# A four-layer block on one core: index tiles loaded ahead of tokens and weights, the tokens of the first two chunks of phase two normalized in SBUF, and first-phase times chosen anew

## The chip, the cores and the metric

One Trainium2 chip, of which the kernel uses one core. The metric is the time of one execution in microseconds (us) on the device; the time of a kernel is the median of its runs. The engines of the core are named as in the profile: PE (matrix products), PEld (PE's weight loads), DVE (vector), ACT (scalar), POOL (GpSimd) and SP (whose queue issues most of the transfers).

## The reference

Four layers over 4096 tokens of 512 channels (two sequences of 2048), each with a layernorm in front and a residual addition behind:

```python
x = x + attn_a(_layernorm(x), W_rvk, W_out, time_decay, time_first)
x = x + ffn(_layernorm(x), lut, gate_idx, up_idx, down_idx)
x = x + mamba(_layernorm(x), in_proj_w, conv_w, conv_b, x_proj_w, dt_proj_w, ...)
x = x + ffn(_layernorm(x), lut, gate_idx, up_idx, down_idx)
```

- `attn_a`: r, v, k = x W_rvk. A scan over the tokens of a sequence keeps, for each channel, a running maximum o and two weighted sums p and q; its output is (A p + B v) / (A q + B) with A and B exponentials of differences to the maximum. The result is sigmoid(r) times that output, times W_out.
- `ffn`: silu(x G) * (x U), times D, where G, U (1376 x 512) and D (512 x 1376) are given as 4-bit indices into a table `lut` of 16 numbers.
- `mamba`: x is projected to 1024 channels and 1024 gates; the channels pass a causal convolution of 4 taps and silu (u); x_proj gives 128 numbers for the step size and 16 each for B and C; delta = softplus(dt_proj); for each channel and each of 16 states h = h exp(delta A) + delta u B, y = sum over states of h C, plus u D; times silu(gate), times out_proj.

## The kernel before

**Two phases.** Phase one (pool context `pa`) does the attention of all tokens in 8 chunks of 512 tokens (TA). Each has 4 channel blocks, so there are 32 units, and each unit ends with the operation `y` (L460 and L461). Phase two (`pb`) does the other three layers in 16 chunks of 256 tokens (TB). Each chunk has a period of 32 slots (SLOTS), one for each pair of 512-element scans (L872). The tokens pass from phase one to phase two through memory, in the tiles `x1d`, which L353 stores and `load_x` (L583) fetches.

**The order is written out by hand.** A `Line` collects steps with a time each and emits them sorted by that time; no scheduler reorders them, so an engine's queue is the order of these times. In phase one the times stand in the dictionary `AA`, in units; `t + AA["y"]` is the place of `y` of unit t. In phase two they stand in `AT`, in slots of chunk w from `t = 32 * w`; w = -1 prepares chunk 0. `Stream` lays the weight tiles of phase two, 18 buffers, 8 slots ahead. Transfers are issued by SP's queue in the order of the program, and an issue that waits holds up those behind it.

**Lookups in phase one.** The feed-forward weights come as 11 tiles of 128 x 1536 indices, and each tile's numbers are looked up once and stored to memory (`wff`).

- Three tiles go through PE: `ix` is loaded (L202), cast to bf16 by ACT (L207, `ixb`); for each of 16 values DVE marks where it stands (L211, tile `one`, three buffers), and PE adds nine products of the mark with `pieces` (L218), which are the table's value, split in three bf16 parts, times the identity. ACT makes the 48 pieces (L193), ahead of everything in the order.
- Eight tiles go through DVE alone by bit arithmetic, 23 operations each (`lookup`, L148 to L177): masks `m` from the index bits, then ands and exclusive ors with the columns of `poly`, into `t` (two buffers), with `g` beside it.

The bits are spread over units -3.02 to 29.13, the marks over -4.09 to 10.75. The attention's own operations on DVE (scans L398, L421, L422; products L401, L420, L425; `y`) stand in between.

**Loads at the start** (SP, in order): lut, the two time columns (L96, L97), the first 512 tokens (L109, 1 MB), the four parts of wrvk (L111), wout (L112), the first `ix` (L202), the first bit tile `m3` (L148).

**The first feed-forward of chunk 0** is done within phase one (`feed_forward`, L282 to L319): it fetches the first 256 tokens from `x1d` into `fx`, normalizes them, and runs the eleven weight tiles through gate and up (PE), silu (ACT), a product (L308, DVE) and down (PE, L313). L318 adds the result, and L319 stores it to `x1d`.

**The passage.** The last channel block's `y`, the output products (L347), the last additions (L351), the stores (L353, L319); then phase two loads its small tensors (L518: conv weights and bias, step bias, D, A_log; the rates from A_log by L519 and L520), `x_proj` (wxp) and `dt_proj` (wdt), in_proj weights (L574) and chunk 0's tokens (L583). It normalizes them (`ln`, L601 to L619), makes the front products (L712), convolution and silu (L722 to L738), the x product (L752; its copies are `bcs` and `dtl`, L755, L757; `bcs` goes through the memory tile `bcd` to be broadcast, L759 and L835), the step sizes (`step_size`, L776 to L815, four quarters of two channel blocks each), gates (L842, L848), decay (L862, ACT), growth (L852, POOL) and the scans (L872), of which POOL folds the states (L882). Chunk 1's first feed-forward ("g1", L659) runs in w = 0, with its own load and layernorm of chunk 1's tokens, placed 5.01 slots before chunk 0's scan begins.

The two entry points of the operations that the change moves are these lines, the loads and the first bit tile:

```python
            line.at(times[0] - 1.0, load)
            line.at(ts[0] - (0.35 if i == 0 else 8.5 * (bt[1] - bt[0])), run, steps)
        ...
            if w == 0:
                line.at(t + AT["g1ln"] - 1.0, load_x, 1)
        ...
            if w == -1:
                line.at(t + AT["frontln"] - 3.0, load_x, 0)
```

Of the kernel before, what the change touches and what calls it, by code (L numbers as in the profile page):

```python
# [8 lines left out]
F32 = mybir.dt.float32  # L9
I32 = mybir.dt.int32  # L10
# [5 lines left out]
P = 128  # L16
# [44 lines left out]
def block_kernel(ctx: ExitStack, tc: tile.TileContext, a: dict, out: bass.AP):  # L61
# [20 lines left out]

    with ExitStack() as pa:
        wpool = pa.enter_context(tc.tile_pool(name="a_w", bufs=1))
# [5 lines left out]
        lp = pa.enter_context(tc.tile_pool(name="a_lut", bufs=1))  # L90
# [17 lines left out]
        first = xp.tile([P, TA // P, C], F32, tag="x", name="x")  # L108
        nc.sync.dma_start(first, a["x"][:TA, :].rearrange("(j p) c -> p j c", p=P))  # L109
        for k in range(KC):  # L110
            nc.sync.dma_start(wrvk[:, k, :], a["w_rvk"][k * P : (k + 1) * P, :])  # L111
        nc.sync.dma_start(wout, a["w_out"].rearrange("(k p) d -> p k d", p=P))  # L112

# [4 lines left out]
        for k in range(4):  # L118
# [5 lines left out]
        AA = dict(k=-1.258, r=-0.633, v=-0.836, head=-1.029, sig=-0.383, top=-0.977, e1=-0.75,  # L124
                  e2=-0.62, state=-0.495, vb=-0.271, car=-0.075, num=0.253, den=0.229, rec=0.247,
                  y=0.413, x=-3.46, stats=-3.029, stat=0.083, each=0.062, copy=0.119, fmul=0.867,
                  opened=-3.355, mean=-2.71, scale=-2.177, turn=-2.106, out=3.964, outs=0.02,
                  add=0.188, bits=(-3.02, 29.13), marks=(-4.09, 10.75), ahead=0.503, ff=(11.44,
                  31.66), ffln=10.705, fgate=0.559, fdown=2.36, times=0.284)
# [10 lines left out]
        def lookup(i):  # L140
# [18 lines left out]
            t = it("t", 2)  # L159
# [24 lines left out]
        wide = wpool.tile([P, NLUT], F32, name="wide")  # L184
        V.tensor_copy(rest, lut)
        pieces = wpool.tile([P, 3, NLUT, P], BF16, name="pieces")
        for q in range(3):
            piece = wpool.tile([P, NLUT], BF16, name=f"piece{q}")
            V.tensor_copy(piece, rest)
            V.tensor_copy(wide, piece)  # L190
            V.tensor_tensor(rest, rest, wide, ALU.subtract)
            for j in range(NLUT):
                S.activation(pieces[:, q, j, :], ident, AF.Copy, scale=wide[:, j : j + 1])  # L193

        def lookup_pe(i, times):
# [13 lines left out]
            def mark(j):  # L209
                box[j] = lp.tile([P, 3 * C], BF16, tag="one", name="one", bufs=3)  # L210
                V.tensor_scalar(box[j], box["ixb"], float(j), None, ALU.is_equal)  # L211
# [9 lines left out]
            def take():  # L221
                t = lp.tile([P, 3 * C], I32, tag="t", name="t", bufs=2)
                for b in range(3):
                    S.copy(t.bitcast(F32)[:, b * C : (b + 1) * C], box["w"][b])
                nc.sync.dma_start(wff[i], t.bitcast(F32))

            line.at(times[0] - 1.0, load)
# [6 lines left out]
        def layernorm(t, n, rows_of, box):  # L234
# [30 lines left out]

            line.at(t + AA["mean"], mean)
            for j in range(n):
                d = AA["each"] * j
                line.at(t + AA["stats"] + AA["stat"] * j, stats, j)
                line.at(t + AA["scale"] + d, scale, j)  # L270
                line.at(t + AA["turn"] + d, turn, j)
                line.at(t + AA["turn"] + d + AA["copy"], copy, j)

        def feed_forward(order, times):
# [41 lines left out]
            def close():  # L316
                for j in range(nj):
                    V.tensor_tensor(box["x"][:, j, :], box["x"][:, j, :], box["po"][j], ALU.add)  # L318
                nc.sync.dma_start(x1, box["x"])  # L319

            line.at(AA["ffln"] + AA["stats"] - 0.5, load)
            layernorm(AA["ffln"], nj, lambda j: box["x"][:, j, :], box)
            for n, t in enumerate(times):
# [4 lines left out]
                line.at(t + AA["fdown"], down, n)  # L328
            line.at(times[-1] + AA["fdown"] + 0.1, close)

        def chunk(ci, t):
# [18 lines left out]
            def add(j):  # L350
                V.tensor_tensor(box["x"][:, j, :], box["x"][:, j, :], box["po", j], ALU.add)  # L351
                if j == TA // P - 1:
                    nc.sync.dma_start(x1d[ci].rearrange("(j p) c -> p j c", p=P), box["x"])  # L353

            if ci:
                line.at(t + AA["x"], load)
            else:
                box["x"] = first
# [110 lines left out]

        cars = {}  # L470
# [11 lines left out]
        for i in range(NBITS):  # L482
            steps, ts = lookup(npe + i), bt[NSTEP * i : NSTEP * (i + 1)]
            line.at(ts[0] - (0.35 if i == 0 else 8.5 * (bt[1] - bt[0])), run, steps)
# [8 lines left out]
    with ExitStack() as pb:  # L493
# [4 lines left out]
        tp = pb.enter_context(tc.tile_pool(name="b_T", bufs=4))  # L498
# [13 lines left out]
        cw = wpool.tile([P, ND, KCONV], F32, name="cw")  # L512
        cb = wpool.tile([P, ND], F32, name="cb")
        dtb = wpool.tile([P, ND], F32, name="dtb")
        dcol = wpool.tile([P, ND], F32, name="dcol")
        acol = wpool.tile([P, ND, NS], F32, name="acol")
        for tl, nm in ((cw, "conv_w"), (cb, "conv_b"), (dtb, "dt_b"), (dcol, "D"), (acol, "A_log")):
            nc.sync.dma_start(tl, a[nm])  # L518
        S.activation(acol, acol, AF.Exp)  # L519
        V.tensor_scalar(acol, acol, -1.0, -1.0 / TINY, ALU.mult, ALU.min)  # L520
        hst = wpool.tile([P, ND, NS], F32, name="hst")
        h0 = wpool.tile([P, ND, NS], F32, name="h0")
        G.memset(hst, 0.0)
# [513 lines left out]
```

## Time and profile before

| | |
|---|---|
| median of 3 runs | 3670.57 us (3670.43 to 3672.81) |
| the profiled execution's own time | 3668.55 us |
| its span in the profile | 3666.7 us |
| PE busy | 3389.0 us, 92% |
| DVE busy | 3215.8 us, 88% |
| POOL busy | 3015.4 us, 82% |
| ACT busy | 2744.4 us, 75% |
| first mark (L211) starts | 21.36 us |
| first `y` (L461) starts | 80.2 us |
| last output addition (L351) ends | 704.2 us |
| first front product (L712) starts | 727.85 us |
| first scan (L872) starts | 789.85 us |

How to read the profile: it is one execution, and its times count from the span's start. A busy share is the time in which an engine executes; issuing transfers and waiting are not in it. The rows of slices cut the span in 40 parts of 91.7 us, and each digit is the busy share of one in tenths. A row of a group gives line, engine, operation, output and inputs with shapes, count, then busy time and mean duration, then the idle time that stood before the group's instructions and what ended it. A row of the order of events gives start, length and the same names.

### The profile page before, as it was taken

How to read it: one execution, taken by the hardware profiler on the slowest of the kernel's cores; microseconds unless marked ns; L12 is line 12 of the kernel's file. 1: busy time of each engine (PE TensorE's matmuls, PEld its weight loads, DVE VectorE, ACT ScalarE, POOL GpSimd, SP SyncE). 2: the span in 40 equal slices, each digit the busy share in tenths (PEclk: the TensorE clock that was granted, in tenths of full speed). 3: DMA queues.
4: the chain of work that ended last, by engine and by line, in shares of the span. 5: the costliest groups of instructions: out<-in, count | busy, mean ns of one | idle time of the engine just before them, and what ended most of it. 6: DMA issues, size and time to landing. Idle time of an engine off the chain costs nothing. (4 is left out here: it accounts for less than half of the span.)

```text
span 3666.7 us, 43341 instructions
## 1 busy us (share of the span) xinstructions
PE 3389.0 (92%) x12577; PEld 2292.7 (63%) x12592; DVE 3215.8 (88%) x4880; ACT 2744.4 (75%) x4870; POOL 3015.4 (82%) x2801
## 2 busy tenths in 40 slices
PE   7898999777999999999999999999999999998698
PEld 3443444365676767676767666676767676766475
DVE  7999999459898989999999999999989898989882
ACT  5566776487787878787888878787878787878661
POOL 2555666358999999999999999999999999999850
PEclk9999999898999999999999999999999999999799
DMA  2121111244656565565656565656565555554441
GB/s 112 41 72 66 58 66 66 89 164 139 192 185 190 183 189 184 179 203 166 216 169 206 168 213 167 209 177 200 176 204 179 190 184 190 187 187 136 137 147 60
DMA packets 266876, 572.49 MB, mean 156 GB/s; under 512 B 29840, under 2 KB 31504, under 8 KB 266640
## 3 DMA queue, kind: packets, MB, share of 16 engines
q1 hardware_dynamic: 266640, 569.73, 47.9%
q8 instruction: 101, 1.65, 0.2%
q14 instruction: 135, 1.11, 0.1%
HBM read 543.14 MB, written 26.48 MB: 155 GB/s over the span
## 5 line engine op out<-in xcount | busy, mean ns | idle before, releaser
L872 DVE TENSOR_TENSOR_SCAN h<-h,db 128x512 f32<-128x512 f32 x1024 | 1252.2, 1223 | 124.1 <-ACT h L862 100.1
L852 POOL TENSOR_TENSOR db<-du,bc 128x1024 f32<-128x1024 f32 x512 | 1206.3, 2356 | 37.1 <-PE y L896 35.5
L862 ACT ACTIVATE h<-dl,acol 128x256 f32<-128x256 f32 x2048 | 955.4, 475 | 302.7 <-DVE hst L875 265.1
L873 DVE TENSOR_TENSOR db<-h,bc 128x512 f32<-128x512 f32 x1024 | 708.0, 691 | 35.9
L882 POOL TENSOR_TENSOR db<-db 128x512 f32<-128x512 f32 x480 | 609.4, 1270 | 0.0
L639 PE MATMUL po<-w,hT 128*128 128x512 f32 x1364 | 600.6, 592 | 0.0
L659 PE MATMUL pg<-xnT,w 128*128 128x256 f32 x2480 | 555.2, 381 | 1.8 <-ACT xnT L619 1.8
L659 PE MATMUL gu<-xnT,w 128*128 128x256 f32 x2480 | 555.7, 379 | 0.0
L659 PEld LDWEIGHTS pg<-xnT,w 128*128 128x128 f32 x2480 | 472.9, 191 | 69.6 <-ACT xnT L619 6.4
L659 PEld LDWEIGHTS gu<-xnT,w 128*128 128x128 f32 x2480 | 472.3, 190 | 69.0 <-issue 6.7
L639 PEld LDWEIGHTS po<-w,hT 128*128 128x128 f32 x1364 | 259.7, 190 | 286.9 <-issue 271.8
L888 POOL TENSOR_TENSOR acc<-db 128x256 f32<-128x256 f32 x480 | 348.4, 726 | 37.7
L376 PE MATMUL ps<-xnT,wrvk 128*128 128x512 f32 x768 | 347.4, 604 | 11.7 <-DVE e L401 9.9
L862 ACT ACT_TABLE_LOAD x206 | 264.3, 1283 | 3.6
L376 PEld LDWEIGHTS ps<-xnT,wrvk 128*128 128x128 f32 x768 | 148.7, 195 | 183.9 <-issue 162.3
L842 PE MATMUL ps<-xnT,w 128*128 128x256 f32 x1024 | 235.6, 384 | 26.6 <-DMA w<-in_in_proj 13.5
L842 PEld LDWEIGHTS ps<-xnT,w 128*128 128x128 f32 x1024 | 196.3, 193 | 70.9 <-DVE x L643 23.0
L712 PE MATMUL ps<-xnT,w 128*128 128x256 f32 x1024 | 236.1, 391 | 1.4 <-ACT xnT L619 1.4
L639 PE MATMUL po<-w,u 128*128 128x512 f32 x512 | 231.8, 601 | 2.1 <-DVE u L919 2.1
L712 PEld LDWEIGHTS ps<-xnT,w 128*128 128x128 f32 x1024 | 200.8, 198 | 36.4 <-ACT h L862 3.3
L437 POOL TENSOR_TENSOR d<-aa,opq 128x512 f32<-128x512 f32 x32 | 58.2, 1818 | 195.7 <-DVE opq L422 183.5
L732 DVE SCALAR_TENSOR_TENSOR ps<-xin,cw,ps 128x256 f32<-128x256 f32 x384 | 187.1, 488 | 26.0 <-ACT ps L726 15.5
(155 smaller groups left out, 5059.9 us busy)
## 6 DMA issues: line engine op xcount, KB each, us to landing
w<-wff SPq DMA_DIRECT2D x1023, 256.0 KB, 2.7
bc<-bcd SPq DMA_DIRECT2D x256, 512.0 KB, 4.2
w<-in_in_proj SPq DMA_DIRECT2D x256, 256.0 KB, 2.7
w<-in_out_proj SPq DMA_DIRECT2D x128, 256.0 KB, 2.7
wff<-t SPq DMA_DIRECT2D x11, 768.0 KB, 3.9
w<-wff SPq DMA_DIRECT2D x11, 768.0 KB, 4.3
x<-in_x SPq DMA_DIRECT2D x8, 1024.0 KB, 5.2
x1d<-x SPq DMA_DIRECT2D x8, 1024.0 KB, 4.3
```

Source lines behind the costliest of these rows:

```text
L376: PE.matmul(ps, lhsT=wrvk[:, k, lo : lo + P], rhs=chunk["xnT"][:, k, :], start=(k == 0), stop=(k == KC - 1))
L639: PE.matmul(po[j], lhsT=lw[:, j * P : (j + 1) * P], rhs=w[i]["w"][:m], start=(i == 0), stop=(i == n - 1))
L659: PE.matmul(to[:m], lhsT=w[:, k, :m], rhs=box["xnT"][:, k, :], start=(k == 0), stop=(k == KC - 1))
L712: PE.matmul(ps[cp][:, j, :], lhsT=wj[:, k, :], rhs=box["xnT"][:, k, :], start=(k == 0), stop=(k == KC - 1))
L732: V.scalar_tensor_tensor(ps[cp][:, j, :], xin[cp][:, j, i : i + TB], cw[:, c, i : i + 1], ps[cp][:, j, :], ALU.mult, ALU.add)
L842: PE.matmul(ps[:, j, :], lhsT=wj[:, k, :], rhs=box["xnT"][:, k, :], start=(k == 0), stop=(k == KC - 1))
L852: G.tensor_tensor(d, box["du", half][:, c4, :].unsqueeze(1).to_broadcast([P, 4, TB]), bs[half, q], ALU.mult)
L862: S.activation(h[:, n, :], box["dl", half][:, c4, :], AF.Exp, scale=acol[:, 4 * half + c4, col : col + 1])
L872: V.tensor_tensor_scan(flat(h), flat(h), flat(d[:, two, :]), 0.0, ALU.mult, ALU.add)
L873: V.tensor_tensor(d[:, two, :], h, cs[half, q][:, two, :], ALU.mult)
L882: G.tensor_tensor(d[:, 0:2, :], d[:, 0:2, :], d[:, 2:4, :], ALU.add)
L888: G.tensor_tensor(to, d[:, 0, :], d[:, 1, :], ALU.add)
```

## The change

- **Loads at the start.** The first bit tile (time -9.9 units) and the first index tile (-9.8) are loaded right after the time columns; the first 512 tokens (-9.7), wrvk, wout (-9.6 on) and phase two's small tensors (-9.5) follow. The rates are computed at unit 3.
- **Pieces.** The 48 pieces are no longer made ahead: `place(j)` makes the three of value j at times from -4.5 units on, 0.069 apart, so that the cast stands after the first of them.
- **Buffers of phase one.** `one` has 2 buffers (3 before), `t` of the bits has 1 (2 before), and a PE lookup's result goes back into its index tile. Pool `a_lut` is opened ahead of the other pools of phase one.
- **Times of phase one.** All of `AA` is chosen anew: `den` at -0.133 units (0.229 before), output products 4.08 (3.964), their additions 0.096 later (0.188), bits from -4.21 (-3.02), scaling 0.191 after the mean (0.533), feed-forward from 13.35 (11.44).
- **Hand-over.** A pool `head` that both phases share holds two tiles `ready` (and the small tensors). Phase one normalizes and transposes chunk 1's tokens into `ready[1]` (at unit 7.821, with a load of its own from `x1d`). It normalizes chunk 0's, after its feed-forward's last addition, out of `fx` into `ready[0]`. The last silu, the last product with D, the additions, the statistics and the scaling stand ahead of or beside the last output products; the transposes come behind these. The stores of `fx` and of the last 512 tokens are issued by ACT's queue instead of SP's.
- **Phase two.** Chunk 0's front and chunk 1's first feed-forward take `ready` and skip their own load and `ln`; `front` writes its normalized tokens into `ready[ci % 2]` from then on, and the pool `b_T` has 2 buffers (4 before). wxp and wdt are loaded at the time of the first front product. Chunk 0's tokens, for the residual, are loaded at slot 0. Chunk 0's front, x product and step sizes have times of their own (`fronta`, `xa`, `step0a`); `g1`, `g1s`, `late` and `step1a` are new. All other times of `AT` stay.

The diff, cut:

```diff
+    head = ctx.enter_context(tc.tile_pool(name="head", bufs=1))
+    ready = [head.tile([P, KC, TB], F32, name=f"ready{i}") for i in range(2)]
+    cw = head.tile([P, ND, KCONV], F32, name="cw")
...
     with ExitStack() as pa:
+        lp = pa.enter_context(tc.tile_pool(name="a_lut", bufs=1))
         wpool = pa.enter_context(tc.tile_pool(name="a_w", bufs=1))
...
-        AA = dict(k=-1.258, r=-0.633, v=-0.836, head=-1.029, sig=-0.383, top=-0.977, e1=-0.75,
-                  e2=-0.62, state=-0.495, vb=-0.271, car=-0.075, num=0.253, den=0.229, rec=0.247,
-                  y=0.413, x=-3.46, stats=-3.029, stat=0.083, each=0.062, copy=0.119, fmul=0.867,
-                  opened=-3.355, mean=-2.71, scale=-2.177, turn=-2.106, out=3.964, outs=0.02,
-                  add=0.188, bits=(-3.02, 29.13), marks=(-4.09, 10.75), ahead=0.503, ff=(11.44,
-                  31.66), ffln=10.705, fgate=0.559, fdown=2.36, times=0.284)
+        AA = dict(k=-1.197, r=-0.758, v=-0.813, head=-1.135, sig=-0.532, top=-0.981, e1=-0.692,
+                  e2=-0.655, state=-0.546, vb=-0.419, car=-0.275, num=0.236, den=-0.133, rec=0.222,
+                  y=0.475, x=-3.69, stats=-2.901, stat=0.11, each=0.061, copy=0.089, fmul=0.561,
+                  opened=-3.107, mean=-2.389, scale=-2.198, turn=-2.092, out=4.08, outs=0.018,
+                  add=0.096, bits=(-4.21, 29.2), marks=(-4.03, 10.79), ahead=0.472, ff=(13.35,
+                  31.01), place=-4.5, places=0.069, ffln=11.025, nextln=7.821, flast=1.489,
+                  turned=2.527, fgate=0.173, fdown=2.314, times=0.273)
...
-            t = it("t", 2)
+            t = it("t")
...
-            for j in range(NLUT):
-                S.activation(pieces[:, q, j, :], ident, AF.Copy, scale=wide[:, j : j + 1])
+        def place(j):
+            for q in range(3):
+                S.activation(pieces[:, q, j, :], ident, AF.Copy, scale=wide[:, q, j : j + 1])
...
-                box[j] = lp.tile([P, 3 * C], BF16, tag="one", name="one", bufs=3)
+                box[j] = lp.tile([P, 3 * C], BF16, tag="one", name="one", bufs=2)
...
-            line.at(times[0] - 1.0, load)
+            line.at(times[0] - 1.0 if i else -9.8, load)
...
-        def layernorm(t, n, rows_of, box):
+        def layernorm(t, n, rows_of, box, at_once=False):
...
+            if at_once:
+                at = dict(mean=0.05, each=0.02, stats=0.0, stat=0.01, scale=0.06, turn=AA["turned"], copy=0.001)
+            else:
+                at = AA
...
-                nc.sync.dma_start(x1, box["x"])
+            def store():
+                S.dma_start(x1, box["x"])
+
+            def load_next():
+                nxt["x"] = lp.tile([P, nj, C], F32, tag="fx", name="fx")
+                nc.sync.dma_start(nxt["x"], x1d[0][TB:, :].rearrange("(j p) c -> p j c", p=P))
+
+            nxt, out_ = {"xnT": ready[1]}, {"xnT": ready[0]}
+            line.at(AA["nextln"] + AA["stats"] - 0.5, load_next)
+            layernorm(AA["nextln"], nj, lambda j: nxt["x"][:, j, :], nxt)
...
+            end = times[-1] + AA["flast"]
+            layernorm(end, nj, lambda j: box["x"][:, j, :], out_, True)
...
-                line.at(t + AA["fdown"], down, n)
-            line.at(times[-1] + AA["fdown"] + 0.1, close)
+                line.at(end - 0.02 if n == NF - 1 else t + AA["fdown"], down, n)
+            for j in range(nj):
+                line.at(end - 0.01, close, j)
+            line.at(end + 2.0, store)
...
-                    nc.sync.dma_start(x1d[ci].rearrange("(j p) c -> p j c", p=P), box["x"])
+                    (S if ci + 1 == NTOK // TA else nc.sync).dma_start(x1d[ci].rearrange("(j p) c -> p j c", p=P), box["x"])
...
+            line.at(t + AA["x"] if ci else -9.7, load)
...
+        for k in range(KC + 1):
+            line.at(-9.6 + 0.01 * k, load_w, k)
+        line.at(-9.5, load_small)
+        line.at(3.0, rates)
+        for j in range(NLUT):
+            line.at(AA["place"] + AA["places"] * j, place, j)
...
-            line.at(ts[0] - (0.35 if i == 0 else 8.5 * (bt[1] - bt[0])), run, steps)
+            line.at(ts[0] - 8.5 * (bt[1] - bt[0]) if i else -9.9, run, steps)
...
-        tp = pb.enter_context(tc.tile_pool(name="b_T", bufs=4))
+        tp = pb.enter_context(tc.tile_pool(name="b_T", bufs=2))
...
-                  scale=0.19, turn=0.82, g1ln=-5.01, g1=0.94, g1s=1.17, late=7.66, step1a=-5.72,
-                  ahead=12.53, spread=2.01, gsilu=0.64)
+                  scale=0.19, turn=0.82, g1ln=-5.01, g1=-0.28, g1s=1.51, late=8.22, step1a=-6.29,
+                  ahead=12.53, spread=2.01, gsilu=0.64, bca=-1.73, step0a=22.65, fronta=(-0.27, 2.4,
+                  1.42, 4.18), xa=14.67)
...
-            ln(t_ln, ci, box)
+            if ci == 1 and layer == 0:
+                box["xnT"] = ready[1]
+            else:
+                ln(t_ln, ci, box)
...
-            ln(t_ln, ci, box)
+            box["xnT"] = ready[ci % 2]
+            if ci:
+                ln(t_ln, ci, box, ready[ci % 2])
...
-                    line.at(th + 4 * q - 4.0, load, half, q)
+                    line.at(th + 4 * q - 4.0 - AT["bca"] * (ci == 0 and half == 0 and q < 2), load, half, q)
...
             if w == -1:
-                line.at(t + AT["frontln"] - 3.0, load_x, 0)
+                line.at(t + AT["fronta"][0] - 0.5, load_w)
+                line.at(t + SLOTS, load_x, 0)
```

## The prediction

> **What bounds the kernel now.** I read the page first, then busy time by stretch, then the order of events at the two seams that the change touches: the start, and the passage from phase one (attention, with the lookups of the feed-forward weights) to phase two (the scan).
>
> ```profile
> span 3666.7 us, 43341 instructions
> PE 3389.0 (92%) x12577; PEld 2292.7 (63%) x12592; DVE 3215.8 (88%) x4880; ACT 2744.4 (75%) x4870; POOL 3015.4 (82%) x2801
> DVE  7999999459898989999999999999989898989882
> POOL 2555666358999999999999999999999999999850
> ```
>
> The DVE row dips in slice 8, which covers 642 to 733 us, and POOL there and in the next: a seam between two full stretches. Busy time by stretch (columns: stretch, length, PE, PEld, DVE, ACT, POOL, granted TensorE clock, DMA share, GB/s):
>
> ```profile
> 0.00:704.20 704.20, 628.02 (x1796) 299.05 (x1812) 636.27 (x633) 445.23 (x689) 398.51 (x236) 0.97 0.18 66
> 704.20:789.85 85.65, 44.66 (x183) 34.63 (x182) 22.09 (x45) 48.45 (x86) 19.42 (x27) 0.76 0.45 159
> 789.85:905.00 115.15, 91.29 (x347) 65.80 (x346) 105.93 (x176) 92.78 (x167) 95.61 (x77) 0.91 0.45 152
> 905.00:1090.00 185.00, 180.53 (x722) 132.20 (x721) 169.10 (x281) 152.74 (x276) 175.96 (x169) 1.00 0.58 187
> ```
>
> Phase one (to 704.2, the end of the last addition, L351) has DVE busy 636 of 704 us; its waits in the middle, 60 to 650 us, come to about 13 us. From 704.2 to the first scan (789.85) no engine is busy even 60%: a chain of single steps. From 905 on PE has 180.5 of 185 us, and a 256-token chunk takes 176.5 us (the fetches of B and C start at 1031.68, 1208.11, 1384.53). The change leaves that part's times alone, so if its start moves, the end moves as far, to first order. So I price three stretches: phase one, the seam, and chunk 0's scan (789.85 to 905).
>
> **The start.** DVE's order of time:
>
> ```profile
> 21.36 1.50 DVE L211 TENSOR_SCALAR one<-ixb 128x1536 bf16<-128x1536 bf16 x3 [7.08 <-ACT ixb L207]
> 25.48 0.56 DVE L211 TENSOR_SCALAR one<-ixb 128x1536 bf16<-128x1536 bf16 x1 [2.62 <-PE lk L218]
> 27.42 0.56 DVE L211 TENSOR_SCALAR one<-ixb 128x1536 bf16<-128x1536 bf16 x1 [1.38 <-PE lk L218]
> ```
>
> DVE idles until 21.4 us: the index tile (L202) is issued tenth, behind 1 MB of tokens and 4 MB of weights, and lands 14.3 us after its issue, at 19.9; the cast on ACT takes 1.47. The change issues the two index tiles (0.79 MB each) fourth and fifth. The transfers ran at about 410 GB/s from 8 us on and had moved 2.44 MB by 10 us, with x (1 MB) landed at 7.8. So the tiles land near 7 and 9 us, and the first mark comes near 10.6 instead of 21.4. ACT's 48 pieces (4.78 us per 16) now stand mostly behind the cast and are wanted three at a time, each mark's nine products being 1.9 us of PE against 0.9 for three pieces; hidden, and without that cover 0.9 us a mark at most, 14 us. x lands near 11.5, the weights near 20; k's first product needs them at about 46 and is covered.
>
> Not all 10.8 us are kept. `one` has two buffers instead of three, so a mark waits for the products of the mark before last: at 0.21 us a product I count four such waits, 5 us. My count of DVE's queue puts the first y at 81.2 us (80.2 before), but with 26 bit steps ahead of it instead of 20, and block 1's state already done. A bit step is 1.88 us (160 of them take 300 us between 80 and 650), so 6 x 1.88 = 11.3; the state (two scans of 1.27, a product of 0.68) 3.2; less 1.0: **13.5 us** less to do.
>
> **Phase one's body.** Added on DVE: statistics of chunk 1's tokens, 2 x (0.68 + 0.18) = 1.7, and the decay rates, 0.23: 1.9 us, on the path. The rest of that layernorm (ACT 2 x 0.81 + 2 x 0.58, eight transposes on PE of 0.27, four small POOL operations) lies beside DVE's work; without that cover it is about 5 us. SP issues one load more. L518's five small loads, taken from the seam, now follow wout in a queue that is idle then. What no row shows is the tightness: two buffers of `one`, one of `t`, and a mean-to-scale gap of 0.19 units (some 4 us) where POOL's four operations took 5.3 (32.61 to 37.93). While marks run, to 309 us, PE is busy 212 of 228 us and DVE 222, so waits can add up. Below: a better order takes some of the 13 us of waits, -4. Above: 32 later marks x 0.4 us, about 12. I take +5, near the sum of the two waits at the start, 4.0. `den` moved ahead of v's products, and the output product later by 0.12 units, change places in queues with one answer: inside those bounds.
>
> Phase one: -13.5 + 1.9 + 5 = **-6.6 us** (from -16 to 0).
>
> **The seam.** Events in order (start, length, engine, line, operation; the bracket is the idle time before it):
>
> ```profile
> 703.52 0.69 DVE L351 TENSOR_TENSOR x<-x,po 128x512 f32<-128x512 f32 x1 [2.75 <-PE po L347]
> 705.95 0.38 SPq L319 DMA_DIRECT2D x1d<-fx  x1
> 710.52 3.45 SPq L574 DMA_DIRECT2D w<-in_in_proj  x6
> 714.36 1.65 SPq L583 DMA_DIRECT2D x<-x1d  x2
> 720.48 0.69 DVE L601 BATCH_NORM_STATS2 st<-x 128x6 f32<-128x512 f32 x1 [7.48 <-DMA x<-x1d]
> 725.03 2.15 PE L618 MATMUL tr<-ident,xn 128*128 128x128 f32 x8 [19.83 <-ACT xn L613]
> 727.85 0.79 PE L712 MATMUL ps<-xnT,w 128*128 128x256 f32 x1 [0.67 <-ACT xnT L619]
> ```
>
> The tokens go out to memory (705.95), come back (714.36, landing 6.1 later), and only then are normalized, transposed and multiplied (727.85). After the change chunk 0's layernorm is taken from `fx` in place while PE makes the last output blocks (26 records, 13 us), so its statistics, scaling and POOL part have cover; the transposes (2.2 us) and the copies (2 x 0.58) follow at once. What is late next is a **transfer**: the first phase-two weights lie in memory that phase one's tiles held, and their issue on SP waits for the landing of the store of `fx`, now issued on ACT's queue behind the store of the last tokens, which waits for L351's last addition. Addition ends 704.2, two issues of 0.4 make 705.0, and these two stores landed 4.2 and 4.0 after their issues; closer together here, I take 4.9, and `fx` is out near 709.9. So the first weight is issued near 710.2, hardly earlier than 710.52. But wxp and wdt (1.15 MB) no longer stand before it, nor x between: two tiles of 0.26 MB are there near 714. Front product at 714 instead of 727.85: -13.9. The last silu on ACT stands ahead of the last sigmoid: +0.6. Behind the store on ACT only the two copies are queued, which wait for PE anyway. -13.3 (from -8, with the weights' 6.0 us median landing and 2 us of delay, to -15).
>
> The clock: from 708 to 726 us the granted clock is 0.50, and the first sixteen front products take 5.46 us where the next take 3.45 (their copies, L722, start at 733.31 and 736.76). PE rests again between 708 and 714, so I take the cold start as unchanged; kept warm, it gives 2.0 us more.
>
> From `dtl` to the first scan (754.60 to 789.85, 35 us) ACT is the chain. Two of its groups there (count, busy, mean ns, idle before):
>
> ```profile
> L784 ACT ACT_TABLE_LOAD x4 | 5.1, 1283 | 0.1
> L790 ACT ACT_TABLE_LOAD x4 | 5.1, 1283 | 0.1
> ```
>
> With two for the gates and the decay, ten table loads. The order of the changed program has eight: 2 x 1.28 = 2.6. Chunk 1's layernorm leaves ACT here (2 x 0.29 + 2 x 0.81 + 1.05 = 3.3). Four quarters of step size are run closer together; ACT's waits and separate steps give 1.6 more by my count of the queue. **-7.5** (from -3, if DVE or POOL are next in the chain, to -10). The Trainium skill, "ScalarE: Activation LUTs", What ACT_TABLE_LOAD costs, adds a drain of 1.38 us to each load; by that page two loads would be worth 5.3. In this trace the activation follows 0.01 us after its load ends, so the sum keeps 2.6.
>
> Seam: -13.3 - 7.5 = **-20.8 us** (from -11 to -25).
>
> **Chunk 0's scan.** Its pace is POOL's: a growth of 2.36 and folds of 1.27 and 0.73 make some 4.7 us for two scans, in both programs. Feed-forward of chunk 1 starts 1.2 slots earlier, its layernorm done. Taken at 0 (from -4, as its residual addition stops waiting, to +4, if the front of chunk 1, 0.56 slots later, comes late).
>
> **Sum.** -6.6 - 20.8 + 0 = -27.4. The profiled execution took 3668.55 us, 1.85 more than its span; the runs' median, 3670.57, is 2.0 above it, and I set the gain against the median: **3643 us**.
>
> **Rivals.**
> - *Phase one gives nothing* (the two buffers take back the whole lead): -20.8 alone, 3650. For it: PE at 93% beside DVE at 97%. Against: only 13 us of waits now.
> - *All gains at once*: lead kept (-11.6, no waits), seam -22, scan -4: -38, 3633. Against: nothing in the profile shows slack this even.
> - *The transfer takes the wait's place*: the weights land as late as the tokens did, because ACT's queue puts the store of `fx` behind the other. Then the seam gives the -7.5 alone, phase one -6.6: 3656. The Trainium skill, "DMA: Bandwidth & Descriptors", Issuing engines are not separate DMA queues, says that another issuing engine adds no bandwidth, only issue time; by it moving the stores is worth the 0.8 us of two issues. For the rival: SP's next issue waits on that landing. Against: wxp, wdt and x no longer share the transfer.
> - *Slower: the marks' two buffers.* Place: the 32 marks up to 309 us; each waits for PE, as 25.48 shows with 2.62 us. Break-even is 27.4 / 32 = 0.86 us a mark beyond the body's 5; at 1.2 us it is +38: 3681. Against: with three buffers none waits after 30 us, and block products lie between marks.
> - *It doesn't do what it says*: the front starts earlier but the steady stretch keeps its start because POOL's chain decides, 3664 with phase one alone. Against: nothing on POOL precedes the scan but what the same chain releases.
>
> **Numbers.** Forecast 0.52 (3636 to 3649); phase one nothing 0.15; all gains 0.12; transfer 0.11; slower 0.04; not what it says 0.06. The range 3628 to 3660 leaves out the last two and the tails. A measurement here tells 0.2% (7.3 us) from no change. Faster by more than that: 0.90 (the first four); within: 0.06; slower: 0.04.
>
> **What would show it.** First mark near 10.6 us; first y near 81; last output addition ending near 698; first front product 10 us after it, and waiting for weights; eight table loads before the first scan, that scan about 65 us after the addition (85.65 before); 176.5 us per chunk after that. Idle time of DVE before marks, put down to PE, over 12 us in all would show the body's term wrong; a front product later than 14 us after the last addition, the seam's.

## The result and the profile after

The changed kernel takes 3645.94 us (median of 4 runs, 3644.86 to 3647.87) against 3670.5 before: a ratio of 0.9933, 95% interval 0.9919 to 0.9946, or 24.6 us less, where 27.4 were forecast. Measured once more beside other kernels it had a median of 3648.22 (5 runs, 3642.29 to 3654.34) and a ratio of 0.9940 (0.9928 to 0.9953). The same program differs by several us from run to run, so medians 3 or 4 us apart are not told apart here; landmarks inside a profile are finer.

The page of the changed kernel:

```profile
span 3643.4 us, 43340 instructions
PE 3398.7 (93%) x12592; PEld 2294.4 (63%) x12592; DVE 3231.3 (89%) x4880; ACT 2739.9 (75%) x4862; POOL 2979.1 (82%) x2803
DVE  8999999568999999999999999998989898989882
POOL 2445666378999999999999999999999999999850
```

DVE has more to do in the first slice (8 instead of 7). Busy time by stretch, cut at the same events as before (last addition, first scan):

```profile
0.00:701.30 701.30, 635.08 (x1828) 302.36 (x1828) 655.97 (x644) 451.08 (x697) 361.65 (x246) 0.97 0.18 68
701.30:765.50 64.20, 45.88 (x186) 36.48 (x185) 17.21 (x33) 38.48 (x71) 13.67 (x17) 0.87 0.60 212
765.50:880.00 114.50, 88.02 (x329) 63.16 (x328) 105.72 (x176) 90.70 (x166) 98.95 (x79) 0.87 0.45 152
880.00:1065.00 185.00, 181.44 (x718) 132.06 (x717) 169.06 (x279) 152.41 (x275) 176.00 (x169) 0.99 0.60 186
```

Phase one is 2.9 us shorter (704.2 to 701.3), the seam 21.45 (85.65 to 64.2), and the steady stretch keeps its pace: the fetches of B and C of chunks 2 and 3 start at 1006.70 and 1183.23, 176.5 apart, 25.0 and 24.9 us earlier than before. In phase one DVE is busy 656 us instead of 636, although its idle time fell from 68 to 45; POOL is busy 362 us instead of 399, with ten instructions more.

The start in DVE's order of time:

```profile
10.20 0.56 DVE L223 TENSOR_SCALAR one<-ixb 128x1536 bf16<-128x1536 bf16 x1 [4.28 <-ACT ixb L219]
...
14.85 0.56 DVE L223 TENSOR_SCALAR one<-ixb 128x1536 bf16<-128x1536 bf16 x1 [1.01 <-PE lk L230]
...
16.97 0.56 DVE L223 TENSOR_SCALAR one<-ixb 128x1536 bf16<-128x1536 bf16 x1 [0.69 <-PE lk L230]
...
39.59 0.56 DVE L223 TENSOR_SCALAR one<-ixb 128x1536 bf16<-128x1536 bf16 x1 [2.86 <-PE lk L230]
```

The first mark stands at 10.20 (21.36 before), and the waits for PE are single ones. The seam in order of events:

```profile
700.42 1.04 PE L273 MATMUL tr<-ident,xn 128*128 128x128 f32 x8
...
700.62 0.69 DVE L380 TENSOR_TENSOR x<-x,po 128x512 f32<-128x512 f32 x1 [2.75 <-PE po L376]
701.34 0.39 ACTq L383 DMA_DIRECT2D x1d<-x  x1
701.77 0.52 ACTq L336 DMA_DIRECT2D x1d<-fx  x1
702.33 1.07 ACT L276 COPY ready<-tr 128x512 f32<-128x512 f32 x2 [7.12 <-PE tr L273]
707.12 3.65 SPq L612 DMA_DIRECT2D w<-in_in_proj  x8
...
709.86 10.44 PE L755 MATMUL ps<-ready,w 128*128 128x256 f32 x36 [8.40 <-DMA w<-in_in_proj]
```

Chunk 0 is ready at 703.4, and PE then waits until 709.86 for weights, whose issue on SP (707.12) waited for the store of `fx`: issued at 701.77, it landed at 706.92.

### The profile page after: what moved, and what is told of

Same layout as the page of the kernel before. It is cut to its first block, busy times and chain, and to the rows that moved or that the text cites. A ratio compares the mean times of both kernels' runs of the same rounds, so it can differ in the third digit from the quotient of the medians.

```text
span 3643.4 us, 43340 instructions
## 1 busy us (share of the span) xinstructions
PE 3398.7 (93%) x12592; PEld 2294.4 (63%) x12592; DVE 3231.3 (89%) x4880; ACT 2739.9 (75%) x4862; POOL 2979.1 (82%) x2803
## 5 line engine op out<-in xcount | busy, mean ns | idle before, releaser
L700 PE MATMUL pg<-xnT,w 128*128 128x256 f32 x2400 | 537.0, 381 | 1.1 <-ACT xnT L657 1.0
L700 PE MATMUL gu<-xnT,w 128*128 128x256 f32 x2400 | 537.6, 379 | 0.0
L700 PEld LDWEIGHTS pg<-xnT,w 128*128 128x128 f32 x2400 | 456.7, 191 | 67.5 <-ACT xnT L657 5.5
L700 PEld LDWEIGHTS gu<-xnT,w 128*128 128x128 f32 x2400 | 456.0, 190 | 68.0 <-issue 6.7
L885 PE MATMUL ps<-ready,w 128*128 128x256 f32 x1024 | 235.6, 384 | 29.0 <-DVE x L681 14.5
L755 PE MATMUL ps<-ready,w 128*128 128x256 f32 x1024 | 238.2, 393 | 10.1 <-DMA w<-in_in_proj 8.4
L885 PEld LDWEIGHTS ps<-ready,w 128*128 128x128 f32 x1024 | 195.4, 192 | 73.9 <-DVE x L681 24.4
L755 PEld LDWEIGHTS ps<-ready,w 128*128 128x128 f32 x1024 | 202.0, 199 | 45.8 <-issue 12.0
L775 DVE SCALAR_TENSOR_TENSOR ps<-xin,cw,ps 128x256 f32<-128x256 f32 x384 | 187.1, 487 | 29.9 <-ACT ps L769 19.5
L930 POOL TENSOR_TENSOR db<-db,acc 128x256 f32<-128x256 f32 x240 | 174.8, 729 | 18.8
```

Source lines behind the costliest of these rows:

```text
L700: PE.matmul(to[:m], lhsT=w[:, k, :m], rhs=box["xnT"][:, k, :], start=(k == 0), stop=(k == KC - 1))
L755: PE.matmul(ps[cp][:, j, :], lhsT=wj[:, k, :], rhs=box["xnT"][:, k, :], start=(k == 0), stop=(k == KC - 1))
L775: V.scalar_tensor_tensor(ps[cp][:, j, :], xin[cp][:, j, i : i + TB], cw[:, c, i : i + 1], ps[cp][:, j, :], ALU.mult, ALU.add)
L885: PE.matmul(ps[:, j, :], lhsT=wj[:, k, :], rhs=box["xnT"][:, k, :], start=(k == 0), stop=(k == KC - 1))
```

## The experiments

Two things were open: why phase one kept only 2.9 us, and whether the seam went as told. Theory A: in the new order DVE's own instructions run longer beside POOL. Its rivals: two buffers for the marks make DVE wait for PE, or no order can keep a lead while PE and DVE are both full. For the seam: the front waits for a transfer that waits for a store; against it, that the first scan waits for something else.

Landmarks of the profiled executions in us. Each ratio is to the kernel before on the same chip, whose median was 3669.2 to 3669.7 in the later sessions. "Lengthening" is worked out from DVE's timeline: the sum, over its instructions of phase one, of each one's duration less the shortest of its kind (operation, tile and shape). Whether a kind goes by the output tile alone or by the inputs too moves each value by up to 3 us, and the differences between kernels by up to 2.

| kernel | median (runs) | ratio (95%) | first y | last addition ends | first front product | first scan | lengthening |
|---|---|---|---|---|---|---|---|
| before | 3670.5 (4) | | 80.2 | 704.2 | 727.9 | 789.9 | 84 |
| after | 3645.94 (4) | 0.9933 (0.9919 to 0.9946) | 78.1 | 701.3 | 709.9 | 765.5 | 96 |
| after_again | 3648.22 (5) | 0.9940 (0.9928 to 0.9953) | 77.5 | 700.2 | 708.9 | 764.6 | 96 |
| e1_start | 3659.10 (8) | 0.9974 (0.9964 to 0.9984) | 69.0 | 692.7 | 715.7 | 777.9 | 84 |
| e2_old_core | 3636.45 (4) | 0.9912 (0.9899 to 0.9926) | 74.4 | 696.9 | 705.5 | 760.2 | 79 |
| e3_early_w | 3636.86 (4) | 0.9911 (0.9896 to 0.9927) | 78.8 | 705.1 | 707.2 | 760.5 | 97 |
| e4_sp_stores | 3642.23 (5) | 0.9928 (0.9915 to 0.9940) | 78.0 | 701.1 | 709.6 | 765.3 | 96 |
| e5_less_pool | 3622.64 (4) | 0.9866 (0.9852 to 0.9880) | 78.7 | 677.6 | 686.4 | 742.5 | 60 |
| e6_den_back | 3644.72 (5) | 0.9934 (0.9921 to 0.9948) | 77.4 | 696.8 | 705.4 | 761.1 | 95 |
| e7_both | 3630.48 (4) | 0.9897 (0.9883 to 0.9910) | 75.0 | 695.8 | 697.9 | 752.9 | 79 |
| e8_start_one2 | 3665.54 (11) | 0.9990 (0.9982 to 0.9999) | 75.8 | 701.5 | 724.7 | 786.8 | 84 |
| e9_no_next | 3647.43 (5) | 0.9936 (0.9923 to 0.9950) | 79.2 | 702.1 | 710.7 | 771.7 | 97 |
| e10_best | 3630.05 (4) | 0.9890 (0.9876 to 0.9903) | 74.0 | 694.6 | 696.7 | 751.7 | 79 |
| e11_late_half | 3641.78 (5) | 0.9923 (0.9911 to 0.9935) | 74.7 | 697.4 | 706.0 | 762.3 | 89 |

**The start alone** (`e1_start`, from the kernel before):

```diff
-            line.at(times[0] - 1.0, load)
+            line.at(times[0] - 1.0 if i else -9.8, load)
...
-            line.at(ts[0] - (0.35 if i == 0 else 8.5 * (bt[1] - bt[0])), run, steps)
+            line.at(ts[0] - 8.5 * (bt[1] - bt[0]) if i else -9.9, run, steps)
...
+        for k in range(KC + 1):
+            line.at(-9.6 + 0.01 * k, load_w, k)
+        for j in range(NLUT):
+            line.at(-4.5 + 0.069 * j, place, j)
```

> The kernel before with the start of the change alone: index tiles loaded first, pieces made one value at a time; times, buffers and hand-over as before. Theory A (what the new order of phase one costs is not the start's fault: the same DVE operations run longer beside POOL in the new order): the first mark starts near 10.2 us instead of 21.36, the first y near 71 instead of 80.2, the last addition near 695, the median near 3661 (-10). Rival (PE and DVE are both full while the marks run, so a lead cannot be kept in any order): first y near 71, but the last addition near 701 and the median near 3667.

First y and last addition come 11.2 and 11.5 us earlier, lengthening stays at 84, and the median falls by 10. The old order keeps the start's whole lead; the changed kernel kept 2.9. The rival falls, and the loss belongs to the rest of the change.

**The old times in the changed kernel** (`e2_old_core`):

```diff
-        AA = dict(k=-1.197, r=-0.758, v=-0.813, head=-1.135, ...
+        AA = dict(k=-1.258, r=-0.633, v=-0.836, head=-1.029, ...
```

(all times from `k` to `add` but `fmul`, and `times`)

> The changed kernel with the times of the attention and its layernorm, output products and additions of before; bits, marks, feed-forward, buffers, start and hand-over of the change kept. Theory A: the 12 us by which the same DVE operations ran longer go, the last addition is near 690 instead of 701.3 and the median near 3635. Rival (the tighter buffers of marks and bits cost it): the last addition stays near 701 and the median near 3646. If the old times do not fit the moved feed-forward and bits, new waits make it slower than 3646.

Lengthening falls from 96 to 79, and y of unit 29 stands 10.5 us earlier than in the changed kernel. Of that 4.4 are left at the last addition, where some 11 were expected: units 30 and 31 take 23.9 us against 19.5, and the old times bring back 8.1 us of waits of y for POOL. In phase one DVE is busy 637 us instead of 656 with the same instructions, and idle 60 instead of 45. The median is 9.5 lower (the profiled execution, 3640.07, was the slowest of the four). So the new times of the attention cost time in the body and win some at the end.

The groups that lengthen most, before and then after (line, operation, tiles, count, busy us, mean ns, idle before):

```profile
L211 DVE TENSOR_SCALAR one<-ixb 128x1536 bf16<-128x1536 bf16 x48 | 39.8, 832 | 11.9 <-ACT ixb L207 7.1 <-PE lk L218 4.8
L153 DVE TENSOR_SCALAR m<-m 128x1536 int32<-128x1536 int32 x32 | 34.5, 1077 | 0.1
L164 DVE TENSOR_SCALAR g<-m,poly 128x1536 int32<-128x1536 int32 x24 | 27.6, 1152 | 0.1
```

```profile
L223 DVE TENSOR_SCALAR one<-ixb 128x1536 bf16<-128x1536 bf16 x48 | 44.5, 927 | 11.6 <-PE lk L230 7.3 <-ACT ixb L219 4.3
L162 DVE TENSOR_SCALAR m<-m 128x1536 int32<-128x1536 int32 x32 | 41.6, 1313 | 0.0
L173 DVE TENSOR_SCALAR g<-m,poly 128x1536 int32<-128x1536 int32 x24 | 35.8, 1490 | 0.1
```

The same 104 instructions take 121.9 us instead of 101.9, while the waits are no longer; other groups shorten, so that 12 of the 20 us remain in the sum (84 to 96). One of them in the timeline of the changed kernel:

```profile
65.66 2.67 POOL L470 TENSOR_TENSOR vb<-aa,vb 128x512 f32<-128x512 f32 x1
67.12 1.62 DVE L223 TENSOR_SCALAR one<-ixb 128x1536 bf16<-128x1536 bf16 x1
```

The mark takes 1.62 us instead of 0.56 and ends 0.41 after POOL's product, which itself takes 2.67 and 1.26 at its shortest. Over all 48 marks of the changed kernel, the 22 that no POOL instruction overlaps take 0.55 us each, the other 26 take 1.25 on average; before the change it was 20 at 0.55 and 28 at 1.03. POOL pays less in turn: its six products of a unit take 341 us in all instead of 370, and y waits for POOL 0.7 us instead of 10.1. I read this as time that the new order moved from POOL to DVE. The Trainium skill, "SBUF — State Buffer", Who interferes with whom, says that DVE's `tensor_scalar` in its two-port modes, and its instructions with two inputs in SBUF, contend with POOL for a port pair that one of the two holds for its whole instruction. The row fits that, and the next run tests the cause.

**Less POOL work** (`e5_less_pool`; it leaves out the numerator's addition and its product with sigmoid(r), so its y lacks them):

```diff
-                G.tensor_tensor(vb, aa, vb, ALU.add)
-                G.tensor_tensor(vb, vb, box["sig"], ALU.mult)
```

> The changed kernel that leaves out two of POOL's six products of each unit of phase one (the numerator's addition of v's part and its product with sigmoid(r)); every DVE instruction stays. They are 134 of POOL's 362 us there. Theory A (DVE's operations run longer while POOL computes): the time that DVE's operations take beyond their shortest, 96 us in phase one, falls by about a third, to 60 to 70, and the last addition comes near 672 instead of 701.3. Rival (they run longer for another reason, PE's or ACT's traffic): it stays near 96 and the last addition stays above 695.

No DVE instruction was touched, and its groups are shorter:

```profile
L223 DVE TENSOR_SCALAR one<-ixb 128x1536 bf16<-128x1536 bf16 x48 | 35.9, 748 | 12.7 <-PE lk L230 8.2 <-ACT ixb L219 4.5
L162 DVE TENSOR_SCALAR m<-m 128x1536 int32<-128x1536 int32 x32 | 35.7, 1129 | 0.0
L173 DVE TENSOR_SCALAR g<-m,poly 128x1536 int32<-128x1536 int32 x24 | 32.8, 1368 | 0.1
```

Lengthening falls to 60, and the last addition comes 23.7 us earlier, at 677.6, where 672 was expected. A mark that no POOL instruction overlaps takes 0.55 us here too, but there are 31 of them instead of 22. DVE's operations run longer because POOL computes beside them: shown.

**Which of the times** (`e6_den_back`, `e11_late_half`):

```diff
-                  ... den=-0.133, rec=0.222, ... times=0.273)
+                  ... den=0.229, rec=0.247, ... times=0.284)
```

> The changed kernel with POOL's denominator, and the reciprocal and its product behind it, at the unit times of before (0.229, 0.247, 0.284 instead of -0.133, 0.222, 0.273). If the earlier denominator is what sets marks and masks beside POOL's products: DVE's time beyond the shortest falls from 96 to 80 to 84 us, the last addition comes near 690 and the median near 3636. If it is the whole set of times: it stays near 96, the last addition near 701, the median near 3646.

Lengthening stays at 95 and the median at 3644.72: the earlier denominator alone is not the cause. Its profile's last addition is 4.5 us early, with the same lengthening; the changed kernel's own two profiles differ by 3.1 us at y of unit 6, so that much is not told apart.

```diff
-                  vb=-0.419, car=-0.275, num=0.236, den=-0.133, rec=0.222, y=0.475, ...
+                  vb=-0.271, car=-0.075, num=0.253, den=0.229, rec=0.247, y=0.413, ...
```

> The changed kernel with the second half of a unit alone at the times of before: v's product, carries, POOL's numerator and denominator, reciprocal, y. If POOL's place against the bit steps is set there: DVE's time beyond the shortest near 80 us instead of 96, last addition near 695, the median near 3638. If it is set by the first half of the unit (projections, scans, exponentials) or the layernorm's times: 93 to 98 us, 3645 or above.

89, between the two: this half of the unit accounts for some 7 of the 17 us between 96 and 79. The rest falls to the other half and the layernorm by difference; no run has these alone. Which single time does it stays open.

**Two buffers for the marks** (`e8_start_one2`, from `e1_start`):

```diff
-                box[j] = lp.tile([P, 3 * C], BF16, tag="one", name="one", bufs=3)
+                box[j] = lp.tile([P, 3 * C], BF16, tag="one", name="one", bufs=2)
```

> The kernel before with the start of the change, and two buffers for the marks instead of three. By the prediction's step (two buffers make DVE wait for PE, 5 us or more in the body): DVE waits for PE at marks 10 us and more where the start alone has 4.8, the last addition near 698 instead of 692.7, the median near 3664. By theory A (buffers cost little, lengthened operations cost the rest): waits at marks up to 8 us, the last addition within 2 us of 692.7, the median 3659 to 3661.

DVE's waits at the marks, for the start alone and then with two buffers (us, times, longest):

```profile
DVE one L207 <- PE lk L214: 4.8, 3, 2.6
```

```profile
DVE one L207 <- PE lk L214: 16.3, 8, 5.0
```

The median rises by 6.4. Here the prediction's step holds and theory A's word on the buffers falls. But 13.9 of the 16.3 us lie ahead of 80 us, at the start: the first y moves by 6.8 us, the last addition by 8.8. In the changed kernel all waits for PE at the marks come to 7.3 us (4.7 in its second profile). There eleven bit operations stand between the marks at 10.20 and 32.66 us, while in this run the first bit operation starts at 21.39; that this is the reason is likely, not shown. Three buffers in the changed kernel were not tried.

**The weights' memory** (`e3_early_w`):

```diff
+        rpool = pa.enter_context(tc.tile_pool(name="a_r", bufs=1))
         lp = pa.enter_context(tc.tile_pool(name="a_lut", bufs=1))
...
-        wrvk = wpool.tile([P, KC, 3 * C], F32, name="wrvk")
+        wrvk = rpool.tile([P, KC, 3 * C], F32, name="wrvk")
...
+        wsp = pb.enter_context(tc.tile_pool(name="b_ws", bufs=NWS))
         wpool = pb.enter_context(tc.tile_pool(name="b_w", bufs=1))
         xp = pb.enter_context(tc.tile_pool(name="b_x", bufs=8))
-        wsp = pb.enter_context(tc.tile_pool(name="b_ws", bufs=NWS))
```

(`pieces` likewise in `rpool`)

> The changed kernel with wrvk and the pieces in a pool of their own, over which the weight tiles of phase two lie: the first weights then wait for the last projection and no longer for the landing of the store of fx. Theory (the front waits for a transfer that waits for that store): weights issued near 675 instead of 707.1, first front product near 703.5 instead of 709.9, with the granted clock still up, so first scan 6 to 8 us after less: near 758, and the median near 3639. Rival (the front is not what the first scan waits for): first front product early, first scan at 765 and the median at 3646.

Its order of events:

```profile
685.07 3.65 SPq L613 DMA_DIRECT2D w<-in_in_proj  x8
...
704.40 0.69 DVE L381 TENSOR_TENSOR x<-x,po 128x512 f32<-128x512 f32 x1 [2.74 <-PE po L377]
...
707.23 9.12 PE L756 MATMUL ps<-ready,w 128*128 128x256 f32 x41 [1.99 <-ACT ready L277]
...
711.04 0.59 ACT L766 COPY xin<-ps 128x512 f32<-128x512 f32 x1 [3.87 <-PE ps L756]
```

Weights are issued 20 us ahead of the last addition, and the front product comes 2.1 us after that addition's end, waiting for the copies of `ready`, instead of 8.6. The first sixteen products take 3.81 us (707.23 to 711.04) against 6.21 in the changed kernel (709.86 to 716.07): PE rested 2 us instead of 8.4. The stretches around the front's start, in the changed kernel and then here (PEclk, the granted clock, is the third number from the end), show the difference:

```profile
705.00:710.00 5.00, 0.14 (x1) 0.17 (x2) 0.00 (x0) 0.00 (x0) 0.00 (x0) 0.50 0.65 218
710.00:715.00 5.00, 5.00 (x13) 3.99 (x14) 0.00 (x0) 0.00 (x0) 0.00 (x0) 0.52 0.94 328
```

```profile
705.00:710.00 5.00, 3.01 (x16) 2.46 (x15) 0.09 (x1) 1.07 (x2) 0.00 (x0) 1.00 0.81 301
```

The seam is 55.4 us instead of 64.2, 8.8 less, and the median 9 lower, although this profile's phase one was 3.8 us longer (it fell back 2.5 us at unit 12, in a part that the edit leaves alone).

**Stores on SP's queue** (`e4_sp_stores`):

```diff
-                S.dma_start(x1, box["x"])
+                nc.sync.dma_start(x1, box["x"])
-                    (S if ci + 1 == NTOK // TA else nc.sync).dma_start(...)
+                    nc.sync.dma_start(...)
```

> The changed kernel with the last two stores issued by SP again. If the issuing engine only costs issue time: first weights 0 to 1 us later than 707.1, the median 3646 to 3647. Rival (ACT's queue in order is what lets the store of fx go early, or holds it): first weights 3 us or more away from 707.1, either way, and the median off by as much.

The first weights are issued at 706.8, the seam is 64.2 us in both, and the ratios' intervals overlap, though the median, 3642.23, is lower than expected: moving the stores to ACT bought nothing that shows.

**Chunk 1's layernorm back in phase two** (`e9_no_next`):

```diff
-            line.at(AA["nextln"] + AA["stats"] - 0.5, load_next)
-            layernorm(AA["nextln"], nj, lambda j: nxt["x"][:, j, :], nxt)
...
-            if ci == 1 and layer == 0:
-                box["xnT"] = ready[1]
-            else:
-                ln(t_ln, ci, box)
+            ln(t_ln, ci, box)
...
-                line.at(t + AT["g1"] - 1.0, load_x, 1)
+                line.at(t + AT["g1ln"] - 1.0, load_x, 1)
```

> The changed kernel without the hand-over of chunk 1: its tokens are loaded and normalized in phase two again, between the step sizes, as before. By the prediction's step (that layernorm took 3.3 us of ACT in the chain to the first scan): from the last addition to the first scan 67 to 68 us instead of 64.2; phase one 2 us shorter for the 1.7 us of statistics; the median 3647 to 3648. Rival (ACT has gaps there, and the layernorm fits in them): 64.2 us, the median 3644.

The two ends of the chain on ACT and DVE, from two answers of its timeline:

```profile
738.20 0.36 ACT L795 COPY dtl<-ps 128x256 f32<-128x256 f32 x1
```

```profile
771.71 1.23 DVE L910 TENSOR_TENSOR_SCAN h<-h,db 128x512 f32<-128x512 f32 x1 [3.52 <-ACT h L900]
```

From `dtl` to the first scan 33.5 us, against 28.4 with the hand-over (737.11 to 765.54) and 35.2 before: the hand-over of chunk 1 is worth 5.1 of the 6.8 us there, more than the 3.3 of its ACT instructions. Chunk 2's fetch of B and C is 4.5 us later than in the changed kernel (1011.21 against 1006.70). The medians, 3647.43 and 3648.22, don't tell 4 us apart.

**Both gains, and the tail** (`e7_both`: the edits of `e2_old_core` and `e3_early_w`; `e10_best`: besides, the new times for the last two units):

> The changed kernel with both edits: the attention's times of before, and wrvk and the pieces in a pool of their own under the weight tiles. If the two gains have separate places they add up: last addition near 697, first front product 2 us later, first scan near 752, the median near 3628. Rival (one takes the other's cover away, or the part behind the first scan sets the end): 3633 or above.

First scan 752.9 and 3630.48 us: 2.5 us short of the 3628 expected, and 39 us below the kernel before on that chip (3669.23). The gains have separate places, but the seam is 57.1 us and not 55.4. PE rested 2.0 us, as in `e3_early_w`, and yet the clock fell:

```profile
695.00:700.00 5.00, 3.01 (x16) 2.47 (x15) 0.69 (x1) 1.07 (x2) 0.00 (x0) 0.88 0.66 248
700.00:705.00 5.00, 5.00 (x19) 4.19 (x19) 0.00 (x0) 1.51 (x4) 0.00 (x0) 0.77 0.64 194
```

The first sixteen products took 5.50 us here (697.92 to 703.42) instead of 3.81. So the early weights do away with the wait of 6.5 us in both kernels, but not always with the cold clock.

```diff
+            B = AN if t >= 30 else AA
...
-                line.at(t + AA[name], fn)
+                line.at(t + B[name], fn)
```

(`AN` holds the changed kernel's times; the last output products and additions take them too)

> Both edits of the kernel that had the attention's times of before and the weight tiles over a pool of their own, and for the last two units and the last output products the changed kernel's times. That kernel needed 23.9 us from y of unit 29 to y of unit 31, the changed kernel 19.5. If the new times are better at the tail alone: 19 to 20 us, last addition near 691, the median near 3626. Rival (the tail's gain needs the units before it): 23 us or more, 3630 or above.

Units 30 and 31 take 23.9 us as in `e2_old_core`, 4.4 us of the lead over the changed kernel are lost in unit 30 (in `e2_old_core` most of it goes in unit 31), and the median is the same: the tail's gain needs the units before it. The two stand as the fastest versions here, both 39 to 40 us below the kernel before and 15 to 16 below the changed one.

> The changed kernel as it is, on the chip of the three others, as their common measure. Every theory: a ratio to the kernel before within 0.0015 of 0.9933, last addition at 701, first scan 64 us after it.

Ratio and landmarks came as expected.

## Why the prediction was right

3643 was forecast, 3645.94 measured, inside the range. By its terms, on the spans (-27.4 forecast, -23.3 measured):

- *First mark*: 10.6 forecast, 10.20 measured. *Lead at the first y*: 13.5 forecast; y came at 78.1 and not 81.2, so by the forecast's own prices it was 11.3 + 3.2 + 2.1 = 16.6, 3.1 more.
- *The body, +5 for tightness*: this is the step that failed. Of the lead of 16.6 us phase one kept 2.9; 13.7 were taken back, 1.9 of them priced as added work, so 11.8 stand where +5 stood. It was also another thing: I priced waits, and DVE's idle time after the first y fell from 41 to 31 us (its wait for POOL at y from 10.1 to 0.7). Summed over DVE's timeline from the first y to the last addition, four things stand against these 10 us. DVE's instructions ran 14 us further beyond their shortest, beside POOL's products (`e2_old_core`, `e5_less_pool`). The feed-forward's last additions and chunk 0's statistics, which stood behind the last addition before, took 3. The decay rates took 1.28 and not 0.23. And the six bit steps ahead of y, priced at 11.3, are 8.1 at their shortest. Together that is 21 us, or 11 of the 11.8 when the 10 are taken off. I had taken a bit step's mean duration, 1.88, as a constant; it depends on the step (0.93 to 1.8 at the shortest) and on what POOL does at that moment. That the forecast's bound above, 12, covered the size is luck: it was worked out for waits at the marks. The forecast's own sign for a wrong term, over 12 us of idle time before marks put down to PE, did not show (7.3).
- *The buffers*: the 5 us of waits at the start came true (5.4 us at the marks ahead of the first y). For the body the price was wrong: 1.9 us of waits at later marks. In the old order two buffers cost 6.4 us of the median, and there too most of the waits lie at the start.
- *The seam, -20.8*: -21.45. The last addition to the front product fell by 15.1 (23.65 to 8.56; forecast 13.3), and PE waits for weights behind the store of `fx`, as said. This 15.1 is read from the order of events; no run takes the hand-over of chunk 0 alone away. The cold start was not unchanged: the first sixteen products took 6.21 us against 5.46. From `dtl` to the first scan -6.8 (forecast -7.5), eight table loads, but the layernorm of chunk 1 is worth 5.1 and not 3.3, so loads and order give 1.7 and not 4.2.
- *Chunk 0's scan, 0*: from the first scan to chunk 2's fetch 241.2 us, 241.8 before. Right. The rest of the span, +1.7, is inside what repeated runs differ by.
- *Rivals*: "phase one gives nothing" came nearest (2.9 of 6.6 us were left). "The transfer takes the wait's place" was half there: it cost 6.5 us of waiting and 2.4 of cold clock, both of which `e3_early_w` took away. "Slower" counted on no wait at a mark after 30 us before the change; there is one, 0.78 us at 46.92.

So the seam was forecast by its mechanism, and it makes most of the gain. In phase one the lead was 3.1 us larger and the loss 6.8 larger than priced; that the two partly cancel is luck.

## What to carry to other kernels

Where two engines lengthen each other's instructions, a new order changes durations as well as waits: sum an engine's busy time per group before and after, not its idle time alone. At a seam, look which memory the first tiles of the next phase lie over; a pool whose last reader is early lets their loads go early, and here that was worth 8.8 us (`e3_early_w`), or 6.2 where the clock fell all the same (`e7_both` against `e2_old_core`). A stretch that a change leaves alone passes a shift of its start on to the end.

## What the runs showed of the hardware

POOL and DVE slow each other by twice and more: a mark of 0.55 us took up to 1.63, a POOL product of 1.26 took 2.67, and with a third of POOL's work gone DVE's same instructions took 36 us less. The profile books this as busy time: DVE's busy time rose by 20 us while its idle time fell by 23. The price of a rest of PE is not a function of its length alone. After 8.4 us (changed kernel) the granted clock stood at 0.50 for 10.2 us and the first sixteen products took 6.21 us; after 8.5 us (`e2_old_core`) for 6.8 us, and 5.17; after 2.0 us it stayed at 1.00 in `e3_early_w`, 3.81, and fell to 0.50 for 3.4 us in `e7_both`, 5.50. What decides it is not shown. One program's runs differed by 12 us (3642.29 to 3654.34).
